# Between a spectral mix and the inverse transform: nine weight slots, other queues for the last stores, loads held behind the sign pass, unread matmuls

## The chip, the cores and the metric

The kernel runs on one core of one Trainium2 chip. All data is float32. The metric is device microseconds of one execution; before the change the median of three runs is 2970.43 us (2969.46 to 2972.65).

The core's engines run side by side, each with a queue of its own: TensorE (PE; its weight loads PEld), VectorE (DVE), ScalarE (ACT), GpSimd (POOL) and SyncE (SP), which here only issues transfers. ScalarE and GpSimd issue transfers too. All transfers run on the same 16 DMA engines.

## The reference

Input x has shape 8 x 32 x 256 x 256 (batch, channel, row, column). Four residual layers follow each other; the change lies inside the first one and at its seam to the rest.

```python
def _L0_conv_ref(x, w1r, w1i, w2r, w2i, bias):
    w1 = w1r + 1j * w1i
    w2 = w2r + 1j * w2i
    x_ft = jnp.fft.rfft2(x)
    out_lo = jnp.einsum('bixy,ioxy->boxy', x_ft[:, :, :M1H, :M2H], w1)
    out_hi = jnp.einsum('bixy,ioxy->boxy', x_ft[:, :, -M1H:, :M2H], w2)
    ...            # the 2 x 32 x 32 modes into a zero spectrum out_ft
    out = jnp.fft.irfft2(out_ft, s=(h, w))
    return out + bias
...
x = x + _L0_conv_ref(_gn(x), w1r, w1i, w2r, w2i, bias)   # 64 x 32 modes of 256 x 129
x = x + _L1_conv_ref(_gn(x), kernel, 1, 2)               # one 5 x 5 kernel for all channels
x = x + _L2_conv_ref(_gn(x), weight_ih, ...)             # recurrence over the columns
x = x + _L3_conv_ref(_gn(x), W, b)                       # running maxima in 4 directions, 1 x 1 mix
```

`_gn` is a group norm over 16 groups of two channels. The spectral weights are 32 x 32 channels for each of 2 x 32 x 32 modes, real and imaginary: 16 MB.

## The kernel before, in words

The kernel is four stages, each written in a hand-made order (`tc.manual_schedule`), so that every engine and every queue works through its instructions as the Python code issues them. The change touches the second half of the first stage and the head of the second.

**Forward pass** (`forward_and_mix`, first part). x comes in 64 units of 1 MB (`xa`, L127, on SP), into a pool `a1x` of `AHEAD` = 7 slots under the tag `xa`. TensorE transforms over columns (yp L142) and rows (sp L169); VectorE and ScalarE make squares and transposes; the normalised modes of all batches stand at the end in one tile `xf`. The weights go into the same slots as x: `load_weights(i)` (L104 to L111) takes the next `xa` slot for one of 16 tiles of 1 MB, 8 KB in each of the 128 partitions, issued on SP. The loads of the first seven tiles are issued in the last iterations of the forward pass, each as its slot comes free, and the constants of the next stage (L48) behind them.

**Mix** (L285 to L324). Eight groups q of four modes in one direction; each takes two weight tiles. For each half tile, 4 x 2 x 2 small matmuls fill two PSUM tiles (mp L297), which VectorE (L308) and ScalarE (L310) copy into a staging tile `stage`, of which there are two (pool `ms`). Behind a half, `load_weights(AHEAD + 2 * q + c)` issues a further weight tile on SP; its slot is the one just used. Behind a group, four stores (L318) of 128 KB take the staging tile to a DRAM tensor `smd`, ordered by mode; so group q + 2 may overwrite its staging tile when the stores of group q have landed. They are on GpSimd's queue for the first seven groups; those of the last group are on SP, GpSimd, ScalarE, SP. At q = 6, SP also issues the first third of x for the first unit of the next stage (xb L356) and six loads of the first batch's spectrum from `smd`, for the rows of the first six groups (L340, L342). Behind the last group come the late rows of the same spectrum (each `late`: one load on SP, two on ScalarE or GpSimd), then the second third of x on GpSimd.

A spectrum tile (`spec`, 8 KB a partition) is loaded twice by halves: once as it is (`own`, L340), once with real and imaginary part swapped (`other`, L342). Spectra have a pool of two buffers, x's thirds a pool of one buffer each; first and second third and the spectra live in pools on the right side of the memory that exist during the mix already, the last third in a pool of the next stage.

**Inverse pass and convolution** (`inverse_and_conv`). At its head (L673 to L691) GpSimd issues the last third of x for unit 0 and SP six loads for the second batch's spectrum. Then the sign pass: half of the swapped part of spectrum 0 is negated by ScalarE (L681) and VectorE (L679). `means` is a small matmul (y L432) and `spectrum` a chain of small VectorE operations. Then the inverse transform over rows (tp L470, copied by ScalarE L477) and over columns (up L487, added to x by VectorE L496) for nine blocks of columns: blocks 0 to 2 need x's first third, 3 to 5 its second, 6 to 8 its last. Each third of the next unit's x is loaded by GpSimd when the third of this unit has been used. From there on the convolution (vp L558) and the transforms of later units are interleaved.

Of the kernel before, what the change touches and what calls it, by code (L numbers as in the profile page):

```python
# [9 lines left out]
F32 = mybir.dt.float32  # L10
AF = mybir.ActivationFunctionType
# [5 lines left out]
P = 128  # L17
B, C, H, W = 8, 32, 256, 256
NG = 16
KM = 32  # L20
EPS = 1e-5
BIG = 3.0e38
AFTER = mybir.DependencyInfo(mybir.DependencyClass.Sync, mybir.DependencyReason.DATA)
A = 4
Q = H // A
# [54 lines left out]
def forward_and_mix(tc, k, d, smd, xmean, keep):  # L80
# [4 lines left out]
    nc = tc.nc  # L85
    CH = 4
    NK = C // CH
    HB = H // 32
    KC = 4
    AHEAD = 7  # L90
    SLICES = 4
    HW = float(H * W)
    with ExitStack() as ctx:
        one = ctx.enter_context(tc.tile_pool(name="m1", bufs=1))
        xp = ctx.enter_context(tc.tile_pool(name="a1x", bufs=AHEAD))


        xf = one.tile([P, KM, KM // KC, 2, B, KC], F32, name="xf")
        wts = {}

        NQ = KM // KC
        KY = KM // 2

        def load_weights(i):  # L104
            if i < 2 * NQ:
                q, h = divmod(i, 2)
                wts[i] = xp.tile([P, 2, KY // 2, KC, C], F32, name=f"wt_{q}_{h}", tag="xa")
                size = KY * KC * C
                nc.sync.dma_start(
                    out=wts[i].rearrange("p h y j o -> p (h y j o)"), in_=d["wm"][q, :, h * size : (h + 1) * size]  # L110
                )  # L111

        with ExitStack() as inner:
# [3 lines left out]
            ps = inner.enter_context(tc.tile_pool(name="a1p", bufs=1, space=PSUM))  # L117
            fh = fwd.tile([P, 2, HB, P], F32, name="fh")
            junk = [fwd.tile([P, 2, 2 * H], F32, name=f"junk_{i}") for i in range(2)]
            units = [(b, n) for b in range(B) for n in range(NK)]  # L120
            zero = fwd.tile([P, B], F32, name="zero")
            xs, ys, sps, squares, exs, turned = {}, {}, {}, {}, {}, {}
# [103 lines left out]
            with tc.manual_schedule(engines=None):  # L226
                k.load("fw")
                for u in range(AHEAD - 1):
                    if u == SLICES:
# [3 lines left out]
                for u, (b, n) in enumerate(units):  # L233
                    if u + AHEAD - 1 < len(units):
                        load(u + AHEAD - 1)
                        if u > 1 and small:
                            k.load(small.pop(0))
                    else:
                        load_weights(u + AHEAD - 1 - len(units))
                    over_columns(u)  # L240
# [14 lines left out]
                    if b == B - 1 and n == NK - 2:  # L255
                        for i in range(SLICES):
                            over_rows(b, i, 0, NK // 2)
                load_weights(AHEAD - 1)
                k.load("gw", "eh", "ident", "ident32", "pair", "valid", "conv")
# [15 lines left out]
                normalise(B - 1)  # L275
                nc.vector.tensor_copy(xmean, xm)

        xp2 = keep.enter_context(tc.tile_pool(name="a2x", bufs=1, side="right", reuse_waits="tile"))
        xb = conv_x(nc, d, [xp2, xp2, None])
        spp = keep.enter_context(tc.tile_pool(name="a2f", bufs=2, side="right", reuse_waits="tile"))  # L280
        spectrum_of = spectra(nc, smd, spp)
        EARLY = slice(0, KC * (NQ - 2))
        sp = ctx.enter_context(tc.tile_pool(name="ms", bufs=2, reuse_waits="tile"))
        ps = ctx.enter_context(tc.tile_pool(name="mp", bufs=4, space=PSUM))
        with tc.manual_schedule(engines=None):  # L285
            for q in range(NQ):
                stage = sp.tile([P, 2, KC, KY, C], F32, name=f"sm_{q}", tag="sm")
                for c in range(2):
                    wt = wts.pop(2 * q + c)
                    for i in range(0, KY // 2, 4):  # L290
                        mps = [ps.tile([P, 4, KC, C], F32, name=f"mp_{q}_{c}_{i}_{s}", tag=f"mp{s}") for s in range(2)]
                        for y in range(4):
                            for h in range(2):
                                for s in range(2):
                                    r, to = slice(64 * s, 64 * s + 64), slice(64 * h, 64 * h + 64)
                                    ky = KY * h + KY // 2 * c + i + y
                                    nc.tensor.matmul(  # L297
                                        mps[s][to, y].rearrange("p j o -> p (j o)"),
                                        lhsT=xf[r, ky, q].rearrange("p r b x -> p (r b x)"),
                                        rhs=wt[r, h, i + y].rearrange("p j o -> p (j o)"),  # L300
                                        start=True,
                                        stop=True,
                                    )
                        for s in range(2):
                            ky = KY // 2 * c + i
                            dst, src = stage[:, s, :, ky : ky + 4], mps[s].rearrange("p y j o -> p j y o")
                            if s:
                                nc.vector.tensor_copy(dst, src)  # L308
                            else:
                                nc.scalar.copy(dst, src)  # L310
                    load_weights(AHEAD + 2 * q + c)
                if q == NQ - 2:
                    xb(0, 0, 0, 0, nc.sync)
                    for early in range(2):
                        spectrum_of(0, early, EARLY, (nc.sync,))
                queues = 4 * (nc.gpsimd,) if q < NQ - 1 else (nc.sync, nc.gpsimd, nc.scalar, nc.sync)
                for m in range(KC):
                    queues[m].dma_start(  # L318
                        out=smd[:, KC * q + m].rearrange("s h r b y o -> (h r b) s (y o)"),
                        in_=stage[m::KC, :, m].rearrange("p s y o -> p s (y o)"),  # L320
                    )
            for late in range(2):
                spectrum_of(0, late, slice(EARLY.stop, KM), (nc.sync, (nc.scalar, nc.gpsimd)[late]))
            xb(0, 0, 0, 1, nc.gpsimd)  # L324

    return xb, spectrum_of


def spectra(nc, smd, pool):
    tiles = {}  # L330

    def load(b, s, x, queues):


        if b not in tiles:
            tiles[b] = pool.tile([P, 2, 2, KM // 2, C], F32, name=f"spec_{b}", tag="spec")
        modes = smd[s, x, :, :, b].rearrange("x h r y o -> x h r (y o)")
        flat = tiles[b].rearrange("p h r y o -> p h r (y o)")
        own, other = (slice(64 * i + KM * s + x.start, 64 * i + KM * s + x.stop) for i in range(2))
        queues[0].dma_start(out=flat[own].rearrange("p h r n -> p (h r) n"), in_=modes.rearrange("p h r n -> p (h r) n"))  # L340
        for ro in range(2):
            queues[-1].dma_start(out=flat[other, :, ro], in_=modes[:, :, 1 - ro])  # L342

    load.tiles = tiles
    return load


def conv_x(nc, d, pools):
    CH = 8
    parts = {}  # L350

    def load(u, b, h, i, queue):
        lo, hi = 3 * i, 3 * i + 3
        for ch in range(2):
            t = pools[i].tile([P, hi - lo, CH, Q], F32, name=f"xb_{u}_{ch}_{i}", tag=f"xb{ch}{i}")
            queue.dma_start(  # L356
                out=t.rearrange("p t c q -> p (t c q)"), in_=d["xl"][b, 2 * h + ch, :, lo * CH * Q : hi * CH * Q]
            )
            for p in range(lo, hi):
                parts[u, ch, p] = t[:, p - lo]  # L360

    load.parts, load.pools = parts, pools
    return load
# [6 lines left out]
def inverse_and_conv(tc, k, d, xmean, x2d, stb, first, xb, spectrum_of):  # L370
# [6 lines left out]
    nc = tc.nc  # L377
    CH = 8
# [8 lines left out]
    with ExitStack() as ctx:  # L387
        wk = ctx.enter_context(tc.tile_pool(name="a2w", bufs=2, reuse_waits="tile"))
        one = ctx.enter_context(tc.tile_pool(name="a2c", bufs=1, reuse_waits="tile"))
        sm = ctx.enter_context(tc.tile_pool(name="a2s", bufs=3, reuse_waits="tile"))  # L390
        xb.pools[2] = ctx.enter_context(tc.tile_pool(name="a2y", bufs=1, reuse_waits="tile"))
        ps = ctx.enter_context(tc.tile_pool(name="a2p", bufs=1, space=PSUM))

        bias = k.bias
# [3 lines left out]
        for i in range(5):  # L398
            t = one.tile([P, NT, CH, Q], F32, name=f"x1_{i}")
            x1s.append((t, t.rearrange("p t (c g) q -> p (t c) g q", c=2)))  # L400

        units = [(b, h) for b in range(B) for h in range(C // (2 * CH))]
        xs, specs, state = xb.parts, spectrum_of.tiles, {}
# [14 lines left out]
        def load_spectrum(b):  # L418

            queue = nc.scalar if b > 1 else nc.sync  # L420
            for s in range(2):
                spectrum_of(b, s, slice(0, KM), (queue,))

        def turn(b, engine):
            t = specs[b]
# [25 lines left out]
        def load(u, i):  # L451
            xb(u, *units[u], i, nc.gpsimd)
# [218 lines left out]

        n = len(units)
        with tc.manual_schedule(engines=None):  # L673
            load(0, 2)
            load_spectrum(1)
            for y in range(2):
                half = specs[0][64:128, y, 1]
                if y:
                    nc.vector.tensor_scalar_mul(half, half, -1.0)  # L679
                else:  # L680
                    nc.scalar.activation(half, half, AF.Copy, scale=-1.0)  # L681
            spectrum(0, means(0))
            for u in range(2):
                begin(u)
# [2 lines left out]
            for p in range(NT):  # L687
                transform(0, p)
                if p in FIRST:
                    i = FIRST.index(p)  # L690
# [691 lines left out]
```

## Time and profile before

| | us |
|---|---|
| Median of three runs | 2970.43 |
| Profiled execution | 2974.49 |
| its span, first to last instruction | 2972.2 |
| Forward pass, TensorE's last sp matmul | to 201.4 |
| Mix, first mp matmul to last staging copy | 207.87 to 255.69 |
| Last store of `smd` landed | 261.9 |
| Sign pass begins | 271.6 |
| First tp matmul | 273.2 |
| Inverse pass and convolution | to about 952 |

The profile is one execution. A row of the chain is start, length and what ran; a row of waits is total us, times and longest; a row of windows is the stretch, then busy time and instructions of PE, PEld, DVE, ACT and POOL, the granted TensorE clock, the DMA share and GB/s. Names as L297 are lines of the kernel. Float32 matmuls stand as two instructions each.

### The profile page before, as it was taken

To read this page: it belongs to the slowest core of one execution; us is meant where nothing else is said; L and a number is where in the kernel's file an instruction comes from. 1 tells how busy PE (TensorE), PEld (TensorE's weight loads), DVE (VectorE), ACT (ScalarE), POOL (GpSimd) and SP (SyncE) were. 2 spreads that over 40 slices of the span, in tenths; PEclk is the share of its full clock that TensorE was granted. 3 is DMA by queue.
4 is the path that set the end of the run, shared out by engine and by line. 5 is a ranking of instruction groups with operands and counts; after the bars stand their busy time and mean duration, and the time that the engine had idled before them with its cause. 6 is when DMAs were issued, how large, how long until landed. Compare 5 with 4: busy or idle time off the path is not lost.

```text
span 2972.2 us, 109934 instructions
## 1 busy us (share of the span) xinstructions
PE 2763.3 (93%) x46840; PEld 1633.9 (55%) x46840; DVE 2567.8 (86%) x5124; ACT 1893.3 (64%) x4469; POOL 897.2 (30%) x1275
## 2 busy tenths in 40 slices
PE   8985999999998999999999999999999588888887
PEld 5664444444454666666666666666666233333333
DVE  6753888888886899999999999999999999999997
ACT  4653677667776888888888888888887222222222
POOL 0112121222212655555555555555555200000000
PEclk9998999999998999999999999999999799999999
DMA  9988677777775676677667766776665698888885
GB/s 399 379 311 274 210 226 225 230 224 228 236 218 146 143 160 141 141 162 161 142 139 162 161 141 141 160 163 139 142 160 128 218 367 332 325 324 322 322 334 228
DMA packets 425891, 651.39 MB, mean 219 GB/s; under 512 B 279176, under 2 KB 283160, under 8 KB 398648
## 3 DMA queue, kind: packets, MB, share of 16 engines
q1 hardware_dynamic: 396120, 484.09, 57.1%
q0 software_dynamic: 15856, 80.38, 8.0%
q10 hardware_dynamic: 13424, 79.90, 6.8%
q8 instruction: 367, 6.01, 0.8%
q14 instruction: 124, 1.02, 0.1%
HBM read 371.63 MB, written 272.63 MB: 217 GB/s over the span
## 4 chain that ended last, share of the span: by engine, by line
PE 72%; DVE 19%; DMA 4%; issue 3%; ACT 1%; SPq 1%; POOL 0%; DVEq 0%; ACTq 0%; POOLq 0%
PE r L847 14%; PE z L847 13%; PE vp L558 13%; PE ni L847 7%; PE nh L847 7%; PE up L487 5%; DVE rv L1133 4%; PE yp L142 3%; DVE dq L1148 2%; DVE uq L1150 2%; PE tp L470 2%; DVE m L1159 2%; DVE m L1156 2%; DVE m L1153 2%; PE sp L169 2%
## 5 line engine op out<-in xcount | busy, mean ns | idle before, releaser
L855 PE MATMUL z<-hs,weights 64*64 64x256 f32 x4080 | 538.9, 382 | 0.0
L939 POOL TENSOR_TENSOR xw<-xw,hs 128x256 f32<-128x256 f32 x496 | 340.1, 686 | 632.4 <-DVE hs L938 630.9
L855 PE MATMUL r<-hs,weights 64*64 64x256 f32 x4080 | 524.9, 375 | 0.0
L855 PE MATMUL ni<-hs,weights 64*64 64x256 f32 x4080 | 524.9, 375 | 0.0
L1191 ACT ACTIVATE ot<-o,bres 128x512 f32<-128x512 f32 x256 | 155.1, 688 | 493.6 <-PE o L1165 479.0
L591 DVE SCALAR_TENSOR_TENSOR x<-vp,r,x 128x128 f32<-128x128 f32 (+2 forms) x640 | 350.4, 562 | 96.5 <-PE vp L558 85.4
L558 PE MATMUL vp<-x,c_conv 64*64 64x384 f32 (+5 forms) x4608 | 422.7, 491 | 0.4 <-DVE x L591 0.4
L929 ACT ACTIVATE n<-n,bih 128x256 f32<-128x256 f32 x510 | 259.2, 508 | 182.1 <-DVE n L928 182.1
L931 POOL TENSOR_TENSOR a<-zm,xn 128x256 f32<-128x256 f32 x510 | 373.2, 732 | 3.3 <-ACT zm L924 3.1
L847 PE MATMUL r<-hs,weights 64*64 64x256 f32 x2040 | 319.0, 389 | 1.4 <-DVE hs L938 0.4
L1165 PE MATMUL o<-m,wsc 32*32 32x512 f32 x3072 | 225.0, 709 | 97.3 <-DVE m L1159 96.0
L558 PEld LDWEIGHTS vp<-x,c_conv 64*64 64x64 f32 x4608 | 222.3, 132 | 167.8 <-issue 88.9
L847 PE MATMUL z<-xn,weights 64*64 64x256 f32 x2040 | 305.3, 376 | 9.4 <-ACT xn L827 9.4
L847 PE MATMUL nh<-xn,weights 64*64 64x256 f32 x2040 | 305.7, 376 | 0.0
L847 PE MATMUL r<-xn,weights 64*64 64x256 f32 x2040 | 305.3, 376 | 0.0
L847 PE MATMUL z<-hs,weights 64*64 64x256 f32 x2040 | 305.2, 376 | 0.0
L847 PE MATMUL ni<-hs,weights 64*64 64x256 f32 x2040 | 304.8, 375 | 0.0
L827 ACT ACTIVATE xn<-xw,shift,turned 128x256 f32<-128x256 f32 x492 | 288.3, 586 | 0.0
L855 PEld LDWEIGHTS ni<-hs,weights 64*64 64x64 f32 x4080 | 284.5, 133 | 0.3
L923 DVE SCALAR_TENSOR_TENSOR n<-nh,bhh,rs 128x256 f32<-128x256 f32 x510 | 246.2, 483 | 42.7 <-ACT rs L922 28.0
L855 PEld LDWEIGHTS r<-hs,weights 64*64 64x64 f32 x4080 | 280.9, 131 | 0.2
L922 ACT ACTIVATE rs<-r,brz 128x256 f32<-128x256 f32 x510 | 241.7, 474 | 58.3 <-PE r L855 37.3
(176 smaller groups left out, 6240.1 us busy)
## 6 DMA issues: line engine op xcount, KB each, us to landing
xb<-in_xl_dram POOLq DMA_DIRECT2D x94, 768.0 KB, 7.0
xa<-in_xt_dram SPq DMA_DIRECT2D x64, 1024.0 KB
fwd<-fm SPq DMA_DIRECT2D x256, 256.0 KB
out_dram<-ot ACTq DMA_DIRECT2D x64, 1024.0 KB
xw<-x2d SPq DMA_DIRECT2D x248, 256.0 KB
fw<-fwd SPq DMA_DIRECT2D x31, 2048.0 KB
x3d<-xw SPq DMA_DIRECT2D x240, 256.0 KB
x<-x3d SPq DMA_DIRECT2D x30, 2048.0 KB
```

The source lines that it names most:

```text
L558: ins = nc.tensor.matmul(vps[bank][to, :, dst], lhsT=k.conv[r, P : P + 64] if kind == 2 else k.conv[r, o], rhs=pair_of(u, ch, g, lo, hi, s ...
L591: nc.vector.scalar_tensor_tensor(x, src[o], r1[rows, g : g + 1], x, ALU.mult, ALU.add, accum_out=s1[rows, 0, n, ch, g : g + 1])
L827: nc.scalar.activation(norms[bi][:, b, w], raws[bi][:, b, w], AF.Identity, bias=shift[:, b : b + 1], scale=sc[:, 1, b : b + 1])
L847: ins = nc.tensor.matmul(out[r], lhsT=weights[r, kind, gate, :], rhs=src[r], start=start, stop=stop)
L855: ins = nc.tensor.matmul(out[pairs[1 - i]], lhsT=weights[r, kind, gate, :], rhs=prev[r, :, q0 : q0 + Q], start=False, stop=stop,)
L922: rs = nc.scalar.activation(r, p["r"], AF.Sigmoid, bias=brz[:, 0:1])
L923: nc.vector.scalar_tensor_tensor(m, p["nh"], bhh[:, 2:3], r, ALU.add, ALU.mult)
L929: nc.scalar.activation(m, m, AF.Tanh, bias=bih[:, 2:3])
L931: product = nc.gpsimd.tensor_tensor(a, zm, cur, ALU.mult)
L939: nc.gpsimd.tensor_tensor(raw, raw, new, ALU.add)
L1165: nc.tensor.matmul(banks[bi][b2][i][32 * j : 32 * j + 32].rearrange("p (w q) -> p w q", q=Q), lhsT=wsc[q, b2, t, :], rhs=src[j][q, b2], st ...
L1191: nc.scalar.activation(ot[:, i], banks[bi][b2][i], AF.Identity, bias=bres[:, b2, i : i + 1])
```

## The change

- `AHEAD` is 9 in place of 7: the pool `a1x` has nine slots, for x and for weights.
- A weight tile is two halves of 4 KB a partition with 32 unused bytes between them, so that one load writes two rows of 4 KB in each partition.
- The last group's stores are on ScalarE, GpSimd, ScalarE, GpSimd.
- Behind the last group TensorE gets eight matmuls of 128 x 128 by 512 columns over the last staging tile, into a PSUM tile `idle` that nothing reads.
- The second and the last third of unit 0's x and the second spectrum are loaded on SP and wait for ScalarE's half of the sign pass (`turned`). The second third of x and the odd spectra move to pools of the second stage; the pool on the right side keeps the first third and the even spectra.

```diff
-    AHEAD = 7
+    AHEAD = 9
...
-                wts[i] = xp.tile([P, 2, KY // 2, KC, C], F32, name=f"wt_{q}_{h}", tag="xa")
-                size = KY * KC * C
+                size = KY // 2 * KC * C
+                t = xp.tile([P, 2, size + 8], F32, name=f"wt_{q}_{h}", tag="xa")[:, :, 0:size]
+                wts[i] = t.rearrange("p h (y j o) -> p h y j o", j=KC, o=C)
                 nc.sync.dma_start(
-                    out=wts[i].rearrange("p h y j o -> p (h y j o)"), in_=d["wm"][q, :, h * size : (h + 1) * size]
+                    out=t, in_=d["wm"][q, :, 2 * h * size : 2 * (h + 1) * size].rearrange("p (h n) -> p h n", h=2)
                 )
...
-        xp2 = keep.enter_context(tc.tile_pool(name="a2x", bufs=1, side="right", reuse_waits="tile"))
-        xb = conv_x(nc, d, [xp2, xp2, None])
-        spp = keep.enter_context(tc.tile_pool(name="a2f", bufs=2, side="right", reuse_waits="tile"))
-        spectrum_of = spectra(nc, smd, spp)
+        kept = keep.enter_context(tc.tile_pool(name="a2k", bufs=1, side="right", reuse_waits="tile"))
+        xb = conv_x(nc, d, [kept, None, None])
+        spectrum_of = spectra(nc, smd, [kept, None])
...
-                queues = 4 * (nc.gpsimd,) if q < NQ - 1 else (nc.sync, nc.gpsimd, nc.scalar, nc.sync)
+                queues = 4 * (nc.gpsimd,) if q < NQ - 1 else 2 * (nc.scalar, nc.gpsimd)
...
+            idle = ps.tile([P, 512], F32, name="idle", tag="mp0")
+            for _ in range(8):
+                nc.tensor.matmul(
+                    idle,
+                    lhsT=k.mean,
+                    rhs=stage[:, 1].rearrange("p j y o -> p (j y o)")[:, -512:],
+                    start=True,
+                    stop=True,
+                )
             for late in range(2):
                 spectrum_of(0, late, slice(EARLY.stop, KM), (nc.sync, (nc.scalar, nc.gpsimd)[late]))
-            xb(0, 0, 0, 1, nc.gpsimd)
...
-        xb.pools[2] = ctx.enter_context(tc.tile_pool(name="a2y", bufs=1, reuse_waits="tile"))
+        late = ctx.enter_context(tc.tile_pool(name="a2y", bufs=1, reuse_waits="tile"))
+        xb.pools[1] = xb.pools[2] = spectrum_of.pools[1] = late
...
-            load(0, 2)
-            load_spectrum(1)
-            for y in range(2):
-                half = specs[0][64:128, y, 1]
-                if y:
-                    nc.vector.tensor_scalar_mul(half, half, -1.0)
-                else:
-                    nc.scalar.activation(half, half, AF.Copy, scale=-1.0)
+            halves = [specs[0][64:128, y, 1] for y in range(2)]
+            turned = nc.scalar.activation(halves[0], halves[0], AF.Copy, scale=-1.0)
+            nc.vector.tensor_scalar_mul(halves[1], halves[1], -1.0)
+            for loads in (xb(0, *units[0], 1, nc.sync), xb(0, *units[0], 2, nc.sync), load_spectrum(1)):
+                for ins in loads:
+                    tc.add_manual_dep(ins.ins, turned.ins.name, AFTER, reason="the first spectrum's loads go alone")
```

The helpers `spectra` and `conv_x` return their loads as lists so that the waits can be attached, and `spectra` takes two pools, for even and for odd batches.

## The prediction

> **What bounds the kernel now.** I read the page first, for the shape of the run, then the chain that ended last around the lines of the diff, then the waits there, then two-microsecond windows, and last the DMA queues. TensorE holds 72% of the whole chain, but the diff touches only the passage from the spectral pass to the inverse pass, so the question is which wait ends last between 200 and 300 us. This is the chain in that stretch (start, length, what):
>
> ```profile
> 207.87 10.12 PE mp L297 x256
> ...
> 220.91 9.97 DMA smd<-sm
> ...
> 231.04 20.60 DMA smd<-sm x4
> ...
> 258.19 3.70 DMA smd<-sm
> ...
> 264.11 9.11 DMA spec<-smd
> 273.22 6.32 PE tp L470 x32
> ```
>
> The reader should see that no engine sets this passage: from 220 to 273 us the chain is transfers, first the mix's own stores, then the first spectrum on its way back. Ahead of 208 us the chain is TensorE's matmuls, and from 273 us on it is TensorE and VectorE again. What becomes earlier at 273 us makes everything after it earlier. Who waited there (total us, times, longest):
>
> ```profile
> ACT sm L310 <- DMA smd<-sm: 23.5, 5, 7.8
> DVE sm L308 <- DMA smd<-sm: 21.8, 5, 7.7
> ACT spec L681 <- DMA spec<-smd: 16.0, 1, 16.0
> PE y L432 <- DMA spec<-smd: 13.9, 1, 13.9
> ```
>
> The evictions of the mix wait five times for a staging buffer whose four stores are still under way; then the sign pass waits 16.0 us for the spectrum. The windows (busy per engine, then granted clock, DMA share, GB/s) say why:
>
> ```profile
> 206.00:208.00 2.00, 0.13 (x4) 0.16 (x8) 1.72 (x3) 1.71 (x2) 0.00 (x0) 0.50 0.00 0
> ...
> 222.00:224.00 2.00, 0.00 (x0) 0.00 (x0) 0.00 (x0) 0.00 (x0) 0.00 (x0) 1.00 1.02 420
> 224.00:226.00 2.00, 0.00 (x0) 0.00 (x0) 0.00 (x0) 0.00 (x0) 0.00 (x0) 0.50 0.99 410
> ...
> 240.00:242.00 2.00, 1.73 (x64) 1.73 (x67) 0.84 (x2) 0.40 (x1) 0.63 (x2) 1.00 1.05 438
> ...
> 266.00:268.00 2.00, 0.00 (x0) 0.00 (x0) 0.00 (x0) 0.00 (x0) 0.07 (x2) 0.50 1.07 105
> 272.00:274.00 2.00, 0.79 (x4) 0.60 (x6) 1.03 (x7) 0.20 (x1) 0.00 (x0) 0.50 1.04 312
> 278.00:280.00 2.00, 1.52 (x12) 0.88 (x8) 0.00 (x0) 1.02 (x2) 0.00 (x0) 0.85 1.02 309
> ```
>
> The DMA engines stand idle before the mix (206 to 208), because all seven slots are full; then they are full (420, 438 GB/s) while TensorE waits. At 266 the late rows of the first spectrum share them with x's second and third pieces and the second spectrum. The clock is at half when the inverse pass starts.
>
> **The mix.** I call T the end of the last staging copy, 255.69 us in the timeline. From 211.6 us, when the eighth weight load is issued, to about 252.5, when the sixth set of stores has landed, the DMA moves 9 weight tiles of 1.049 MB, 1.573 MB of x and six sets of stores of 0.524 MB: 14.16 MB in 40.9 us, 346 GB/s. With nine slots two weight tiles are loaded before the mix, in the idle stretch; 12.06 MB are left. At the same 346 GB/s that takes 34.9 us, 6.0 less. At the 386 GB/s that the queue view gives for 222 to 250 us it takes 31.2, 9.7 less. The floor is TensorE: 128 mp matmuls of one group take 3.85 us, eight groups end at about 239 from 207.9, so no more than some 14 can be won.
>
> The rows of 4 KB concern who waits for whom. The queue view for 222 to 250 us:
>
> ```profile
> DMA packets 2150, 10.81 MB, mean 386 GB/s; under 512 B 457, under 2 KB 457, under 8 KB 1343
> ## 3 DMA queue, kind: packets, MB, share of 16 engines
> q1 hardware_dynamic: 1202, 8.14, 73.5%
> q0 software_dynamic: 943, 2.58, 23.2%
> ```
>
> Packets are one weight row of 8 KB on q1 and 4 KB of store on q0 (2.58 MB is 630 of 4 KB, the rest of the 943 are completions). So 23.2% of 16 engines over 28 us is about 0.16 us for each store packet; in 54 to 64 us, where q1 has 512 rows of 8 KB for 100.7%, a row costs 0.31 us. Here the Trainium skill speaks against the edit: "DMA: Bandwidth & Descriptors", Queues, rings and completion order, says that an engine changes queues only at packet boundaries and that a packet typically holds 9 to 17 descriptors. If nine rows went in a turn, halving the row would change nothing for a store between them. The trace has whole packets of one row (the x rows of 6 KB and the spectrum's rows of 2 KB come as single packets too), so I take the row as the turn: beside a full weight queue a store has 4 of 12 KB now and 4 of 8 KB after. A store set of 0.524 MB then takes 2.6 instead of 3.9 us of transfer, 1.3 less, twice hidden by the other buffer; six sets would be worth up to 4 us, the rule's case 0. Because both this and the two slots draw on the same DMA-limited time, I do not add them fully: T is 7 us earlier (bounds 4 and 12), at about 248.7. The price of the shorter rows themselves: two 4 KB packets at 0.16 us against one at 0.31, 3% of some 18 us of weights, 0.5 us, contained in the bounds. SP issues a weight load in 0.33 us and isn't the limit.
>
> Ahead of the mix, nine slots give nothing: from 50 to 190 us TensorE is busy for 9.5 to 10.0 of each 10 us, and its last slot is released when x's last tile is done, before and after. The padding of 32 bytes a half moves no work.
>
> **The tail, from T to the sign pass.** Now: SP is issuing early spectrum loads until 257.35, so its two stores go at 257.47 and 258.14 and land at 261.9, T + 6.2. After: ScalarE issues two at 0.70 us from T + 0.1, GpSimd two at 0.56 from T + 0.5; the last leaves at T + 1.7 and lands, with the 3.1 us that the chain's last store took after its issue, at T + 4.8 (bounds 4.2 and 5.6). GpSimd has the seventh set's four stores (2.2 us) ahead of them; in the trace they clear just in time.
>
> Then four spectrum loads for late rows on SP and ScalarE and two on GpSimd, issued over 2.2 us (ScalarE's pair, 261.98 to 264.21). Now they land at 271.5, 7.3 us later, beside 3.15 MB of x and 1 MB of second spectrum. After, these are held back, and the 0.26 MB go alone: the unloaded price is the 2.7 us median of stores in 248 to 258 us; I take 2.2 to 3.0. So sign pass at T + 9.4 in place of T + 15.9: 6.5 gained (bounds 4 and 7.5).
>
> **What is held back.** Four x loads and six spectrum loads move from GpSimd and SP to SP behind `turned`. SP has nothing else until the first x2d store tens of us later; GpSimd loses four issues of 0.55 us. SP needs 2 x 1.21 us for x and about 4.5 for the six spectrum loads. x's second piece (1.57 MB) should land some 7.5 us after the sign pass (1.3 issue, 1.5 start, 4.4 at 360 GB/s), or 11 if the transfers share badly at the 254 GB/s that 264 to 281 us shows. Its first reader is VectorE's addition for block 3, at 285.6 now, 14.0 after the sign pass (12.2 with a warm clock). So it is hidden by at least 1 us; the third piece lands by +12 to +17 and is read at about +18; the second spectrum by +17, read after 300 us, +30. Unit 1's first piece, issued by GpSimd at 285.3, queues behind at most 3 us of this and has 12 to spare. I cost all at 0; without the cover, one to one.
>
> **Unread matmuls.** 8 calls are 16 passes, as float32 matmuls appear twice (one call at L274 is x2). No full-array 512-column row exists; the nearest is up L487 with eight tiles at once: 32 in 1.95 us, so 0.49 us for a 512-column pass, or 0.54 by 160 in 10.8. Sixteen take 7.8 to 8.6 us at full clock, from T + 0.1 to about T + 8.3, before the spectrum is there at T + 9.4. At half clock 15.6, which would hold the first means back by 6; TensorE was at 1.00 from 232 to 258, so I take full clock. Their worth: tp's 32 passes take 6.3 us at half clock and 4.5 at full (same row, 280 to 300 us): 1.8. Whether the clock holds: PE stops at T + 8.3 and tp starts at about T + 11, 2.7 us. The trace lost the clock 2.6 us after 221.4 and 3.2 after 254.9, and regained it only 5.4 us into tp. The Trainium skill, "TensorE: Matmul & The Clock Gate", What's actually happening, wants an idle window of about 3.4 us, in a grid that doesn't reset; by that the gap passes and the 1.8 are won, by the trace's shortest drop it could be lost. I take 1.5 (bounds -3 and 2).
>
> **Sum.** 7 + 6.5 + 1.5 = 15 us off the profiled execution: 2974.49 (span 2972.2 and 2.3 around it) to about 2959.5. The median of the runs is 4.06 below that execution, so 2970.43 - 15 gives 2955.4.
>
> **Rivals.**
> 1. The mix is paced by the stores' round trip, not by bytes. For: landings at 226.3, 231.0, 238.3, 244.9, 250.4 each release the next evictions, and a store takes 6.4 us at the median. Against: the queue is full meanwhile, and alone stores need 2.7. T moves by 2, total 9: 2961.
> 2. The stores profit fully from the equal turn: T moves by 12, total 20: 2950.
> 3. Slower: a 4 KB weight row costs as much as the 8 KB one, 0.31 us, so the weight stream runs at 210 GB/s. The seven tiles in the mix then need 35 instead of 18 us, and the two early ones delay them further: +17 and +5 against 15, 2977. It decides from about 0.29 us per row. The 0.16 us of store packets speaks against it.
> 4. The change does not do what it says: the clock falls all the same and the held-back loads become the wait that the late rows were, at block 3. Mix gain 7, the rest returned but for 0 to 2: about 2962 to 2966; if the slots also bring nothing, no change.
>
> **How the numbers follow.** A measurement can tell about 0.2%, 5.9 us, from no change. Forecast 0.55, rival 1 0.16, rival 2 0.12, rival 3 0.07, rival 4 0.10, of which half stays within 5.9 us. Faster 0.88, same 0.05, slower 0.07. The range from 2948 to 2965 holds the forecast with its bounds, rival 1 and most of rival 2, and half of rival 4.
>
> **What would show it.** Right: two more weight loads ahead of 197 us and the first one of the mix still at 211.6; evictions' wait for stores well under 23.5 us; last staging copy near 249; sign pass under 10 us behind it; tp in about 4.5 us at clock 1.00. Wrong: weight packets at 0.3 us, a wait of block 3's addition for x, or y L432 waiting for the unread matmuls.

## The result: 0.11% faster, a fifth of the forecast

| | before | after |
|---|---|---|
| Median, first measurement (12 runs each) | 2970.85 us | 2968.24 us |
| Median, second measurement (33 and 19 runs) | 2972.05 us | 2969.02 us |
| Spans of the traced executions | 2972.2, 2971.1 | 2966.1, 2964.8, 2966.0 |

The ratio is 0.9989 (95% interval 0.998 to 0.9998), in the second measurement 0.9988 (0.9981 to 0.9995). The change makes the kernel about 3 us faster, by the intervals 0.6 to 6; 15 were forecast, and the measured time lies above the forecast range. In the traced executions 6.0 us are won. All milestones below are from these traces, two of before and three of after, as means; T is the end of the last staging copy.

| us | before | after | forecast gain | gain |
|---|---|---|---|---|
| First mp matmul to T | 47.2 | 43.8 | 7 | 3.5 |
| T to sign pass | 15.5 | 11.6 | 6.5 | 3.9 |
| Sign pass to first up matmul | 8.2 | 8.4 | 1.5 | -0.2 |
| Start of the first up matmul | 279.5 | 272.8 | 15 | 6.7 |
| Last s matmul of the convolution to the recurrence | 9.9 | 10.6 | 0 | -0.8 |

(The first mp matmul itself begins 0.5 us later in the traces of after; with it the first three rows give the fourth.)

**The mix after.** Waits of the first traced execution of after, 180 to 310 us: engine, line, what was waited for, total us, times, longest.

```profile
ACT sm L310 <- DMA smd<-sm: 13.0, 4, 5.8
ACT sm L310 <- PE mp L297: 12.2, 11, 4.7
ACT spec L692 <- DMA spec<-smd: 11.6, 1, 11.6
PE y L449 <- DMA spec<-smd: 4.0, 1, 4.0
PE mp L297 <- issue: 3.5, 5, 2.0
PE mp L297 <- ACT sm L310: 3.1, 2, 2.8
```

The same view of before has for TensorE:

```profile
PE mp L297 <- ACT sm L310: 12.0, 4, 5.6
PE mp L297 <- issue: 0.3, 1, 0.3
```

The evictions still wait 13.0 us for the stores of a staging buffer (23.5 before). As much again is now waited for TensorE (6.9 before), and TensorE, which waited 12.0 us for the evictions before, now stops for 3.5 us at something that the view only calls issue. The sign pass waits 11.6 us for the spectrum instead of 16.0. The two-microsecond windows of the same execution, with the columns as in the prediction:

```profile
234.00:236.00 2.00, 2.00 (x61) 2.00 (x56) 0.00 (x0) 0.00 (x0) 1.16 (x3) 0.69 1.03 418
...
242.00:244.00 2.00, 1.73 (x49) 1.24 (x40) 1.77 (x3) 1.81 (x4) 0.00 (x0) 1.00 0.72 283
244.00:246.00 2.00, 1.90 (x69) 1.89 (x72) 1.05 (x3) 0.60 (x2) 0.76 (x2) 1.00 0.14 53
...
266.00:268.00 2.00, 2.00 (x12) 1.19 (x10) 0.00 (x0) 0.59 (x1) 0.00 (x0) 0.50 1.02 412
```

And of before:

```profile
248.00:250.00 2.00, 1.39 (x51) 1.14 (x42) 0.00 (x0) 0.00 (x0) 2.00 (x4) 1.00 0.68 271
250.00:252.00 2.00, 0.93 (x30) 0.94 (x34) 1.55 (x3) 1.57 (x4) 0.15 (x1) 1.00 0.37 139
```

The heavy traffic ends in the window 242 to 244 instead of 248 to 250: six us earlier, just what the bytes of two weight tiles were computed to give. But T comes only 3.9 us earlier in this execution, and the mix is 3.5 us shorter in the mean. At 244 to 246 the DMA moves 53 GB/s and TensorE is busy for 1.90 of 2 us: for the last 8 us of the mix the engine and not the bytes is the limit. At 234 to 236 TensorE has lost half of its clock, behind a stop of 2 us inside a half tile.

**The tail after.** The timeline of the same execution (start, length, queue or engine, line, operation, count, idle time before and what ended it):

```profile
251.94 7.11 PE L324 MATMUL idle<-sm,c_mean 128*128 128x512 f32 x16 [0.88 <-DVE sm L308]
...
257.46 1.39 SPq L349 DMA_DIRECT2D spec<-smd  x2
...
263.13 0.63 ACT L692 ACTIVATE spec<-spec 64x512 f32<-64x512 f32 x1 [11.61 <-DMA spec<-smd]
...
264.85 5.64 PE L487 MATMUL tp<-c_eh,spec 128*64 128x256 f32 x32 [1.25 <-DVE stb L466]
```

The late spectrum loads start when the last stores have landed, here T + 5.7, and the sign pass begins 5.7 us after that. The unread matmuls end at 259.05, and the tp matmuls at 264.85 still take 5.64 us: the window 266 to 268 stands at a clock of 0.50.

Rival 3 was that a row of 4 KB costs as much as one of 8 KB. The DMA queues of after, 222 to 242 us:

```profile
DMA packets 2247, 8.31 MB, mean 416 GB/s; under 512 B 344, under 2 KB 344, under 8 KB 2243
q1 hardware_dynamic: 1535, 6.32, 77.1%
```

77.1% of 16 engines over 20 us, by 1535 packets, is 0.16 us for a packet of 4 KB. Rival 3 is false.

### The profile page after: what moved, and what is told of

It reads as the page before. It is cut to its first block, busy times and chain, and to the rows that moved or that the text cites. A ratio compares the mean times of both kernels' runs of the same rounds, so it can differ in the third digit from the quotient of the medians.

```text
span 2966.1 us, 109971 instructions
## 1 busy us (share of the span) xinstructions
PE 2768.3 (93%) x46856; PEld 1635.9 (55%) x46856; DVE 2569.7 (87%) x5124; ACT 1893.1 (64%) x4469; POOL 894.8 (30%) x1272
## 4 chain that ended last, share of the span: by engine, by line
PE 45%; DVE 19%; issue 2%; DMA 1%; ACT 0%; SPq 0%; POOL 0%; DVEq 0%; ACTq 0%
PE r L862 14%; PE z L862 13%; PE ni L862 7%; PE nh L862 7%; DVE rv L1148 4%; DVE dq L1163 3%; DVE uq L1165 2%; DVE m L1174 2%; DVE m L1171 2%; DVE m L1168 2%; PE o L1180 2%; DVE top L1156 1%; PE r L870 1%; PE z L870 1%; PE ni L870 1%
## 5 line engine op out<-in xcount | busy, mean ns | idle before, releaser
L862 PE MATMUL z<-xn,weights 64*64 64x256 f32 x2040 | 305.3, 376 | 10.6 <-ACT xn L842 10.6
```

The lines of the kernel that those rows point to most:

```text
L862: ins = nc.tensor.matmul(out[r], lhsT=weights[r, kind, gate, :], rhs=src[r], start=start, stop=stop)
```

## Experiments

All durations are from each kernel's traced execution. Timed ratios are against before, with their 95% intervals.

### Both kernels once more

Before and after, unchanged.

> A second profile of the kernel before, unchanged. The first one took 2974.49 us, 3.6 above the median of its runs. Theory A, that this execution was a long one of its kind: the second takes 2970 to 2972, with the mix, the tail and the first up matmul (280.2) within 0.5 us of the first profile, and the difference lies elsewhere, at the seam to the recurrence or in the last stage. Theory B, that the passage itself varies by several us from run to run: the first up matmul moves by more than 2 us.

> A second profile of the changed kernel. In its first profile TensorE stood still twice in the middle of a piece of work with no wait shown (1.1 us in the forward pass at 37 us, 2.0 us in the mix at 231.6, with half the clock for 3.4 us behind it). Theory A, that these are chance hits of instruction loading: they are at other places or gone, the first mp matmul comes at 207.9 and the last staging copy at 248 to 250. Theory B, that the fuller transfer queues cause them each time: first mp at 209 and last copy at 251 to 252 again.

> The changed kernel once more, on the chip of the others. If the passage's 7 us are what a run gains, its median is 4 to 7 us under that of the kernel before; rival, that something later gives most of them back and the first measurement's 2.6 us is all: 2 to 3 us.

Before: 46.6 us from the first mp matmul to T, sign pass at T + 15.1, span 2971.1. After: 43.3 and 45.3; T + 11.9 and T + 11.5; spans 2964.8 and 2966.0. The mix of after stands unchanged in five further kernels or repeats below (those that touch only the tail); these took 42.7 to 43.3 us, so 45.3 is the outlier of eight, and the mix gains 3.5 us by the three traces of after, 4.0 by all eight. The stop of 2 us inside the half tile did not come again at its place: the longest of its kind are 0.8 and 0.4 us in the repeats.

### Rows of 8 KB, and seven slots

```diff
-                t = xp.tile([P, 2, size + 8], F32, ...)[:, :, 0:size]
+                t = xp.tile([P, 2 * size], F32, ...)          # rows8k, nine slots
```
```diff
-    AHEAD = 9
+    AHEAD = 7                                                 # slots7, rows of 4 KB
```

> The changed kernel with weight rows of 8 KB again, all else as changed. Theory of the prediction, that a row is the turn in which the weight queue and the stores alternate: with twice as long a row a store set takes 1 to 2 us longer, evictions wait longer for stores (toward 20 us in place of 13.0), the last staging copy is 2 to 4 us later than with 4 KB rows. Rival, that the order does not depend on the row: the last staging copy and the waits stay within 1 us.

> The changed kernel with seven slots, rows of 4 KB and all else as changed. Theory of the prediction, that two more tiles loaded in the idle stretch ahead of the mix save their transfer time: last staging copy 3 to 6 us later than with nine slots. Rival, that the mix is paced by the stores' round trip and by TensorE alone: within 1.5 us. And if the forward pass's 1.2 us later end came from the deeper queue of loads, the first mp matmul is back at 207.9 here.

With rows of 8 KB the mix takes 45.8 us. From its waits, 180 to 310 us:

```profile
ACT sm L310 <- DMA smd<-sm: 22.2, 5, 7.0
```

With seven slots and rows of 4 KB: 45.4 us, store waits of 19.5 us; the three traces of after have store waits of 13.0 to 15.0. Each half of the edit alone leaves the mix 1.4 to 1.8 us shorter than before, by one trace each, against 3.5 to 4.0 for both. With rows of 8 KB the trip of a group's stores, first issue to the release of the next evictions, takes 9.1 to 11.8 us, 10.1 in the mean (10.0 in the two traces of before); with rows of 4 KB it takes 7.4 to 10.1 us in the three traces of after, 9.1 in the mean. (The last groups' stores, with little beside them, are left out.) So the shorter row speeds the stores up by about 1 us a group. Timed, both kernels lie at ratios of 0.9988 (0.9981 to 0.9995) and 0.9989 (0.9983 to 0.9996), beside after's 0.9988: runs don't separate 2 us here, the waits do.

### Three staging buffers

```diff
-    AHEAD = 9
+    AHEAD = 7
-        sp = ctx.enter_context(tc.tile_pool(name="ms", bufs=2, ...))
+        sp = ctx.enter_context(tc.tile_pool(name="ms", bufs=3, ...))
```

> The changed kernel with seven weight slots and three staging buffers, the memory of two slots spent on the third buffer. From the first mp matmul to the last staging copy: 47.8 and 46.7 us before, 42.7 and 43.3 as changed, 45.4 with seven slots. Theory, that the mix is paced by the stores' round trip of 8 to 10 us for each staging buffer: 40 to 42.5 us. Rival, that the bytes ahead of it decide, as the prediction had it: 45 to 46, as with seven slots and two buffers.

No eviction waits for a store any more, and yet the mix takes 45.7 us. Its waits between 205 and 262 us:

```profile
ACT sm L310 <- PE mp L297: 26.8, 32, 4.3
PE mp L297 <- issue: 10.3, 6, 3.5
```

The timeline shows where TensorE stops (the idle time before each run of matmuls stands at its end):

```profile
218.77 3.72 PE L297 MATMUL mp<-wt,xf 64*64 64x128 f32 x127 [1.02 <-issue]
225.94 5.01 PE L297 MATMUL mp<-wt,xf 64*64 64x128 f32 x127 [3.46 <-issue]
232.07 3.72 PE L297 MATMUL mp<-wt,xf 64*64 64x128 f32 x127 [1.11 <-issue]
238.24 5.39 PE L297 MATMUL mp<-wt,xf 64*64 64x128 f32 x127 [2.45 <-issue]
```

With seven slots and no store waits the evictions wait for TensorE. The weights come no sooner than before (last row at 245.1 us, 244.5 before), but TensorE is not seen to wait for them: no wait of an mp matmul for a weight tile stands in the view, and the stops do not lie at the beginning of a tile. They lie 127 matmul instructions apart, 21 to 26 into a group of 128, so at fixed places of TensorE's program. The packet records tell what comes ahead of them. The queue that the profile calls instruction brings a packet of 16 KB about once a group (8 from 205 to 255 us), and the stop of 3.46 us ends 2.3 us after such a packet has begun (223.64 us). That holds for all 46 stops over 0.1 us that are put down to issue in the mixes of all 16 traces: they lie at six such places, each ends 2.2 to 2.6 us after the beginning of a 16 KB packet, and each of these packets began while weights or x were still on the DMA engines. The evidence is that TensorE's next instructions arrive late while the queues are full. No run set this apart from the rest, so why the packets begin late is not shown. Taking the store waits away uncovered these stops, 10.3 us of them.

### Without holding back; without unread matmuls; the old queues for the last stores

```diff
-            for loads in (xb(...1, nc.sync), xb(...2, nc.sync), load_spectrum(1)):   # no_hold
-                ...tc.add_manual_dep(ins.ins, turned.ins.name, ...)
+            xb(0, *units[0], 1, nc.gpsimd)      # ahead of the sign pass
+            xb(0, *units[0], 2, nc.gpsimd)
+            load_spectrum(1)
```
```diff
-            for _ in range(8):                  # no_unread
-                nc.tensor.matmul(idle, ...)
```
```diff
-                queues = ... else 2 * (nc.scalar, nc.gpsimd)                         # old_stores
+                queues = ... else (nc.sync, nc.gpsimd, nc.scalar, nc.sync)
```

> The changed kernel, with x's second and third piece (on GpSimd) and the second spectrum (on SP) issued ahead of the sign pass again, as before the change. If holding them back is what shortened the tail (last staging copy to sign pass 15.9 and 15.1 us before, 11.3 and 11.9 in the changed kernel), the tail is 14.5 to 16 us here and the first up matmul 3 to 4 us later than 271 to 273. Rival, that the new queues of the last stores did it: the tail stays near 12.

> The changed kernel without its eight unread matmuls. From the sign pass to the first up matmul it took 8.6 and 7.8 us before and 8.0 and 8.6 with them, because the clock fell 3 to 5 us behind the last of them, just ahead of the inverse pass. If they bring nothing as they stand, it takes 7.8 to 9 us here too. Rival, that they shorten the warming up: 1 us longer than with them, 9 to 9.6. If they held anything up, the sign pass or the first means would come earlier.

> The changed kernel with the last group's stores on SP, GpSimd, ScalarE, SP, as before the change. From the last staging copy until the late spectrum loads start (all stores landed) it took 6.3 and 5.6 us before, 5.7 and 6.0 as changed; the prediction had 4.8. Theory, that the queue is not what the stores wait for, since the early spectrum loads share the DMA engines with them on any queue: 5.6 to 6.3 us here. Rival, that the new queues do bring the 1.4 us of the prediction and something else took it: 6.8 us or more.

Without holding back, the sign pass begins at T + 14.6, 3 us later than in after. Its late loads again share the engines with x: between 260 and 262 us no engine but GpSimd, which issues loads, has work, and the DMA share is 1.03:

```profile
260.00:262.00 2.00, 0.00 (x0) 0.00 (x0) 0.00 (x0) 0.00 (x0) 1.49 (x5) 1.00 1.03 119
```

Holding back is therefore worth 3 us of the tail. The old queues for the last stores make the landing 0.5 to 0.8 us later (T + 6.5; but before, with these queues too, had T + 6.3 and T + 5.6) and the sign pass come at T + 12.4. Without the unread matmuls the first up matmul follows the sign pass by 8.7 us, with them by 8.0 to 8.7: as the change has them, they bring nothing.

Timed, however, neither undoing is slower than after: no_hold is at 0.9984 (0.9977 to 0.999), no_unread at 0.9983 (0.9977 to 0.999). For no_hold the traces say where its 3 us come back. Its first up matmul is only 1.0 us later than after's, as sign pass to first up takes 7.6 and its T lay early; and from there to the last s matmul it takes 669.1 us, where before takes 670.8 and 671.1, after 671.1, 670.9 and 671.0. The windows around a stall of TensorE near the end of the convolution show the difference. After:

```profile
916.00:918.00 2.00, 0.98 (x8) 0.80 (x12) 1.17 (x5) 1.91 (x7) 0.25 (x1) 0.85 0.82 223
918.00:920.00 2.00, 2.00 (x18) 1.14 (x16) 0.00 (x0) 1.90 (x7) 0.76 (x1) 0.50 0.81 185
```

And no_hold:

```profile
918.00:920.00 2.00, 0.36 (x6) 0.34 (x6) 1.61 (x6) 1.94 (x6) 0.00 (x0) 1.00 0.83 219
920.00:922.00 2.00, 2.00 (x27) 1.40 (x30) 0.16 (x1) 1.87 (x8) 1.01 (x1) 1.00 0.78 174
```

Both stall there; in after the clock falls for 3.4 us behind the stall, in no_hold it doesn't. The same slice of half clock is in both traces of before and all three of after, and is missing in no_hold, both traces of unread12, stages3 and no_early. These five take 669.1 us for the stretch; ten of the other eleven traces take 670.8 to 671.1, and all_late3_warm, which has the slice, 671.4. So 1.8 us hang on how such a stall falls, and none of the edits touches this stage. How it falls can be read from the grid of 3.413 us on which all half-clock slices lie (see "Not expected of the hardware"): in the eleven traces with the slice TensorE was busy for 0.49 of the window ahead of it, in the five without for 0.51 to 0.60 of the least busy window there. For no_unread no place was found where its time comes back.

### Twelve calls in place of eight

```diff
-            for _ in range(8):
+            for _ in range(12):
```

> The changed kernel with twelve unread matmuls in place of eight. Sixteen passes took 7.1 us, so 24 take 10.7 and end about 0.5 us ahead of the first means. If the size of the gap decides, the granted clock stays 1.00 through the tail, the four tp groups take 4.3 to 4.8 us and the first up matmul comes 6.2 to 6.8 us after the sign pass, 2 us sooner. Rival, that these matmuls do not keep the clock or delay the means: no gain, or the sign pass to first up stays over 7.8.

> The kernel with twelve unread matmuls once more, for its time beside the changed kernel's on the same chip. If the 2 us between sign pass and first up matmul are real, it is 1.5 to 3 us faster than the changed kernel; rival, no difference in the medians.

The unread matmuls now take 10.54 us and end at 263.03 and 261.1 us, 1.1 and 1.0 us ahead of the first means. The windows of the first trace:

```profile
264.00:266.00 2.00, 0.59 (x4) 0.54 (x6) 1.43 (x7) 0.63 (x1) 0.00 (x0) 1.00 0.26 37
266.00:268.00 2.00, 2.00 (x20) 1.77 (x20) 0.00 (x0) 0.76 (x2) 0.00 (x0) 1.00 0.85 304
```

The clock stays at 1.00, where after had 0.50. The groups by shape, 260 to 272 us (busy us, mean ns, idle before), after first and unread12 second:

```profile
L487 PE MATMUL tp<-c_eh,spec 128*64 128x256 f32 x32 | 5.6, 529 | 1.2 <-DVE stb L466 1.2
```
```profile
L487 PE MATMUL tp<-c_eh,spec 128*64 128x256 f32 x32 | 3.8, 391 | 1.3 <-DVE stb L466 1.3
```

The first up matmul follows the sign pass by 6.2 us in both traces: 2 us are won, the worth that the prediction gave to the clock. Timed ratios 0.9978 (0.9968 to 0.9989) and 0.9982 (0.9974 to 0.999), of which part may be the 1.8 us at 917 us just told.

### Without the early spectrum loads

```diff
-                    for early in range(2):
-                        spectrum_of(0, early, EARLY, (nc.sync,))
+            nc.gpsimd.memset(spectrum_of.tiles[0], 0.0)       # ahead of the mix
```

> The changed kernel without the six early loads of the first spectrum (its rows of the first six groups stay zero, set by GpSimd ahead of the mix; this leaves out part of the computation). Theory, that the early loads share the DMA engines with the last stores: the stores have landed 4.3 to 5.0 us behind the last staging copy in place of 5.6 to 6.0, and the sign pass begins 9.5 to 10.5 us behind it in place of 11.3 to 11.9. Rival, that stores and late loads have this length by themselves (issue, transfer, completion): 5.5 to 6 and 11 to 12 again.

Timeline, 240 to 275 us:

```profile
255.42 1.34 ACTq L318 DMA_DIRECT2D smd<-sm  x2
...
258.86 1.55 SPq L349 DMA_DIRECT2D spec<-smd  x2
...
264.82 0.63 ACT L692 ACTIVATE spec<-spec 64x512 f32<-64x512 f32 x1 [9.75 <-DMA spec<-smd]
```

T is at 255.4; the stores have landed at T + 3.5 (5.7 to 6.0 in after), and the sign pass begins at T + 9.5. So it was the early spectrum loads that made the last stores late; they are on another queue, and what the two have in common are the DMA engines. Here eight calls are enough: they end 2.05 us ahead of the y matmul, tp takes 3.81 us, and the first up matmul follows the sign pass by 6.1. Its one time is 2963.61 us.

### Nine slots, three staging buffers, all of x held back

```diff
-        sp = ...tile_pool(name="ms", bufs=2, ...)       # AHEAD stays 9
+        sp = ...tile_pool(name="ms", bufs=3, ...)
-                    xb(0, 0, 0, 0, nc.sync)             # x's first third, now held back like the rest
-            for _ in range(8):
+            for _ in range(12):
...
+            y0 = means(0)                               # all_late3_warm alone, from here on
+            for _ in range(3):
+                nc.tensor.matmul(idle_2, lhsT=k.mean, rhs=k.eh, ...)
-            spectrum(0, means(0))
+            spectrum(0, y0)
```

> The changed kernel with three staging buffers beside nine slots, twelve unread matmuls, and x's first piece held back behind the sign pass too, which frees the memory for the third buffer and 1.57 MB of transfer in the mix. With seven slots the third buffer brought nothing, as the bytes held the mix up (45.8 us). Theory, that with nine slots the bytes are out of the way by 240 and the stores' round trip (13 to 14 us of waits left) is the next bound: first mp to last staging copy 38 to 41 us in place of 42.7 to 43.3, sign pass 2 to 4 us sooner, and a total of 2961 to 2964 if x's first piece arrives ahead of the first addition (about 7.5 us behind the sign pass). Rival, that TensorE and its loading of instructions are the next bound: 42 to 43 again. And if the first addition waits for x, the first addition comes over 8 us behind the sign pass and some of the gain is lost.

> all_late3 with three more unread matmuls of 256 columns behind the first means, 1.3 us of work in a gap of 1.6 us ahead of the inverse transform. If the clock fell there only because of the gap, it stays at 1.00, the first up matmul comes 6.2 to 6.5 us behind the sign pass in place of 7.75, and the total is 2961 to 2964, 1 to 2 us under all_late3's 2964.5. Rival, that the fall depends on the place of the window alone: half the clock again, no gain.

The mix takes 41.4 and 42.3 us, the shortest of all. The stores hold up an eviction not at all in the one, and for 3.0 us in the other. TensorE's stops put down to issue are 7.1 and 7.2 us, so the rival, that TensorE and the loading of its instructions are the next bound, comes nearer than the 38 to 41 us that were expected. In all_late3 the clock still fell (265.2 to 268.6 us): the unread matmuls ended at 261.33, 2.6 us ahead of tp. In all_late3_warm three more calls fill that gap; its timeline, 250 to 275 us:

```profile
263.47 1.54 PE L699 MATMUL idle<-c_eh,c_mean 128*128 128x256 f32 x6
264.94 3.82 PE L486 MATMUL tp<-c_eh,spec 128*64 128x256 f32 x32
```

The clock does not fall there, and the first up matmul stands at 269.4, 3.4 us ahead of after's mean. Timed 0.9971 (0.996 to 0.9983) and 0.9963 (0.9949 to 0.9976): all_late3_warm, 2963.16 us, has the lowest ratio of all versions timed, below both kernels.

## Why the prediction was wrong

**What failed first: the mix, 3.5 us for 7 (bounds 4 and 12).** The computed 6.0 us for the bytes were right for the traffic, which ends six us earlier. The step that failed is the one from the bytes to T. It took TensorE as ready whenever weights and buffers are, at full clock down to a floor at 239, and put its own stops at nothing. In these kernels the mix is TensorE's busy time, its two kinds of stop and 0.7 to 0.8 us for the last copy, to 0.1 us:

| us, mean of the traces | mix | TensorE busy | stops behind evictions that wait for stores | stops put down to issue |
|---|---|---|---|---|
| before (2) | 47.2 | 34.9 | 11.1 | 0.4 |
| after (3) | 43.8 | 35.3 | 5.9 | 1.9 |
| stages3 | 45.7 | 34.6 | 0 | 10.3 |
| all_late3 | 41.4 | 33.6 | 0 | 7.1 |

The stops behind the stores fell by 5.2 us, not by 7 or more. Of these, 1.5 came back as stops put down to issue, which the evidence of stages3 ties to the arrival of instructions, and 0.4 as busy time: 3.5 us are left. The three traces of after share the stops in different ways (3.3 and 3.5, 6.5 and 1.7, 7.9 and 0.4 us). Rival 1, that the stores' trip and not the bytes paces the mix, priced T at 2; measured are 3.5 to 4.0, between rival and forecast. It was right that the stores still held the mix up, for 5.9 us. The argument against it, that a store alone needs 2.7 us, was the wrong one: in the mix no store is alone, and a trip of 9 us with weights in flight bounds a loop of two buffers. The floor of 31 us was out of reach: TensorE ran at half clock for 7 to 16 us of the mix in all 16 traces and was busy for 33.5 to 36.2, and where the stores stop it no longer, the other stops remain.

**The turn in the queue.** That the shorter row lets the stores through sooner was right: undone, store waits go back from 13.0 to 15.0 us to 22.2 and the mix is 2 us longer, within the 0 to 4 forecast. The reason given against the Trainium skill ("DMA: Bandwidth & Descriptors", Queues, rings and completion order) does not hold, though: with nine rows in a turn, shorter rows make shorter turns too, so rows8k cannot tell one row from several. The packet records can. From 221 to 226 us in before both queues are full, and where a record begins just as one other ends the two can be taken for neighbours on one engine. Behind a weight row came a store row 86 times, a store's completion (a record of 4 bytes) 46 times and never another weight row; behind a store row came a weight row 31 times and another store row once. So here the turn is one record, as the prediction assumed, and not the page's 9 to 17 descriptors.

**The tail, 3.9 for 6.5 (bounds 4 and 7.5).** Two terms were too small. The landing of the last stores was put at T + 4.8, and is 5.7 to 6.0, hardly sooner than before (5.6 and 6.3); no_early shows why, by T + 3.5 without the early spectrum loads beside them. New queues shorten the issue, but not what the transfer shares with the loads in flight. The late loads were put at 4.6 us, with their issue, and take 5.7 to 6.0, in no_early too, with nothing else under way: the median of stores of 128 KB was the wrong row for six small loads. What sets their length was not tried. Holding back was right in kind (3 us), and x did arrive before its readers.

**Unread matmuls, 0 for 1.5.** They took 7.1 us (7.8 to 8.6 forecast) and so ended at T + 7.2; the spectrum came at T + 11.6 instead of 9.4. The gap to tp, forecast 2.7, became 5.8, and the clock fell, as rival 4 said. The premise was right: no_early's gap of 3.9 us up to tp, with the y matmul in it, keeps the clock and wins 2 us, and so do twelve calls. The length of the gap alone doesn't decide: 2.6 us lost the clock in all_late3. Here the prediction leaned on "TensorE: Matmul & The Clock Gate", What's actually happening. The fixed grid of windows is borne out; the idle window of 3.4 us is not, as the gap of all_late3 is shorter and lost the clock. By the grid, that gap lay in one window, in which TensorE was busy for 0.48; no_early's longer gap was shared by two windows with 0.43 and 0.54 and kept it. The busy share of a window counts, and near one half it is luck on which side it falls. The size was fitted to a tail that was itself a forecast.

**The rest.** 3.5 + 3.9 - 0.2 - 0.5 is 6.7 at the first up matmul. 0.8 is lost at the seam to the recurrence, where the last stores of the convolution on SP end later than its matmuls; why was not tried. The spans differ by 6.0. The timed medians differ by 2.6 and 3.0 us, the ratios by 3.3 and 3.6. The rest of the kernel behind the first up matmul takes 2692.0 and 2692.3 us before, 2694.9, 2691.4 and 2692.1 after, and a single slice of half clock is worth 1.8. Most of the difference between traces and timing lies in which executions were traced: those of before took 3.6 and 0.2 us more than the medians of before beside them (2970.85 and 2972.64), the first and third of after 0.1 more and 1.2 less than theirs. In the mean that is 2.5 of the 2.4 to 3.4 us by which the traces show more than the timing. In which stage the traced executions of before were long stays open.

## What to carry to other kernels

Before pricing the removal of a limit, list every kind of stop of the engine behind it: here half of the stops behind the stores went, and a part came back as stops of TensorE at fixed places of its program, which the view only calls issue. Look up such places in the packet records. Price a transfer at the end of a stage by all that is on the DMA engines then, including the loads that were put there early to save time. Keep-warm matmuls brought nothing here while they left one clock window less than about half busy: size them in the changed kernel, by the wait that is measured there, with something to spare. Before crediting an edit with one or two microseconds, compare the slices of half clock in the whole trace.

## Not expected of the hardware

- Half clock comes in slices on a fixed grid. In each of the 16 traces all edges of the slices lie whole multiples of 3.413 us apart, to 0.02 us; in after they are 207.44 to 214.27, 234.75 to 238.16, 262.05 to 268.88 and 917.41 to 920.83, and no_unread has one of 17.1 us (254.2 to 271.3). Cut into such windows, the traces show what decides: of windows at full clock, the 383 that half clock followed had TensorE busy for at most 0.52 of their length, the 12443 that full clock followed for at least 0.41 (the first 20 us of each trace aside). Between 0.41 and 0.52 both occur; the ends of matmuls are modelled, so the share is not exact. A stall of one or two microseconds therefore costs either nothing or a slice, by how it falls on the grid.
- In the mix of after, too, TensorE stops inside a half tile, with the DMA full (418 GB/s in the window above). The timeline puts it down to nothing but issue, and the half clock follows:

```profile
233.53 5.38 PE L297 MATMUL mp<-wt,xf 64*64 64x128 f32 x127 [1.98 <-issue]
```

It ends 2.3 us after a 16 KB packet of the instruction queue began (231.24 us), and 127 matmuls follow, as in stages3.

- Six loads of 0.26 MB in all take 5.7 to 6.0 us from the first issue to the sign pass with nothing else under way (8.9 beside x in no_hold), longer than a 0.5 MB store set with little beside it, whose trip is 3.9 us in after.
